# Full matrix products issued as 32- or 64-column tiles when the tensor array already stands in that form

## The chip, the cores and the metric

The kernel runs on one core of a Trainium2 chip. The metric is device time in microseconds for one execution, the median of several runs. A core has a tensor engine (PE; its weight loads are listed as PEld), a vector engine (DVE), a scalar engine (ACT), GpSimd (POOL) and DMA queues, of which SP issues most. PE multiplies a stationary operand (up to 128 rows by 128 columns, loaded first) with a moving operand (up to 512 columns). The array can also be addressed as tiles: a stationary operand of 32 rows by 128 columns uses one of four row tiles, one of 128 rows by 32 columns one of four column tiles, and tiles that lie side by side can work at the same time. In the profile's rows the shape of the stationary operand stands after the names, as in `128*32`. That shape, rounded up to 32, 64 or 128 each way, is called the *form* of the array below.

## The reference

Two layers over 2048 tokens (2 sequences of 1024) of 256 numbers, all float32. Each layer is `x = x + s * g`, where s and g are two branches of the normalized x.

```python
x = L0_attn_x
xn = _layernorm(x, axis=-1)
s = _L0_attn_ref(xn, ...)          # 16 heads of 16, 8 shared keys and values, softmax
g = _silu(_L0_ffn_ref(xn, ...))    # gate and up to 688, weights are picks from a table of 16
x = x + s * g
xn = _layernorm(x, axis=-1)
s = _L1_attn_ref(xn, ...)          # recurrence: state = (1 - w) * state + k v, y = r state
g = _silu(_L1_ffn_ref(xn, ...))    # 8 experts of 176, top 2 per token, and a shared one of 352
x = x + s * g
```

## The kernel before

The whole program is one list of small steps. Each step is a letter, and the string ORDER (lines 78 to 100) says by hand in which order the steps are issued; every engine runs its instructions in that order. So PE's work is one fixed sequence, in which products of different stages stand side by side. There is no loop at run time and no scheduler.

*Layer 0, to about 548 us.* Attention works with keys and queries turned so that a head takes a slot of 32 rows. For each unit of work four heads are handled. `largest` (letter m, L309) multiplies query and key in a 32*128 row tile, and DVE takes the largest (L316). `weigh` (w, L340; L332 for the first eight units) makes the scores in row tiles, and ACT takes their exponentials (L344). `gather` (v, L368; L357 for the first) multiplies the exponentials with the values in four 128*32 column tiles, one for each head, all into one PSUM bank. Around them stand full products and transposes: `turn_x`, `turn_k`, `turn_q`, `divide`, `turn_c` (transposes, L207, L255, L287, L386, L401), `qkv` (L218, 512 columns), `project` (L410, 256 columns). POOL meanwhile decodes the picked weights (L270 and L274). Eight PSUM banks are handed out in turn (`bank`), so that a product waits until DVE or ACT has read the bank that it gets. From about 407 us on the feed-forward branch comes in as well: `gate_up0` (L559, and L541 for the last, shared block; 512 columns) and `down0` (L575; 6 products of 256 columns for a block of 128 tokens).

*Layer 1, from about 575 us.* The recurrence is made in blocks of 128 tokens, four to a step n. `project` and `values` (L1132 with 512, L1159 with 256 columns) make its inputs; `diagonal` (L1186) is in row tiles of 64*128; `level` (L1228) does seven doubling steps, each with 128*64 column tiles of 64 moving columns, and between two levels DVE updates the operands rd and kT (L1235, L1241) and folds the results into w (L1266); `states` and the first half of `reads` (L1298, L1324) are 128*64 tiles too, the second half (L1335) is 64*64. `result` (L1351) is a full product. The router's `logits` (L725) are four 128*32 tiles. `gate_up_s` (L750) is the shared expert's gate and up: three blocks of 128, 128 and 96 channels with 512 columns; `down_s` (L1051) its second product, 256 columns. `route` finds for each expert tile who goes there; its step `ids` (L924) is 32 full products of only 39 moving columns, each behind a comparison `at` on DVE (L913, two buffers). Then come 39 expert tiles: fetch (POOL, L963), a transpose (L975), gate and up (L990), a transpose (L1009), down (L1018), and a scatter to memory (POOL, L1031). At the end `collect`, `combine` and `finish` read the scattered rows, add them up on DVE (L1065) and write out.

A float32 product is two matmul records in the profile. The records of a group of tiles that run together start within some 20 ns of one another.

Of the kernel before, what the change touches and what calls it, by code (L numbers as in the profile page):

```python
# [18 lines left out]
P = 128  # L19
# [5 lines left out]
E = 256  # L25
# [36 lines left out]
NFS = len(FS)  # L62

# [10 lines left out]
C_ALL = C_PRIO + NE  # L74

# [27 lines left out]
def attention(  # L103
    nc, tc, st, b0, small, singles, xs, xnT, s_sb, wlut, ident, epst,
# [24 lines left out]
    for k in range(4):  # L129
        nc.tensor.matmul(bank(f"none_{k}"), xnT[:, 0, 0:P], xnT[:, 0, 0:512], start=True, stop=True)  # L130
# [71 lines left out]
    def turn_x(t):  # L202

        ps = bank(f"xnTp_{t}")
        for kc in range(KC):
            for k in range(2):
                nc.tensor.transpose(  # L207
                    ps[:, (2 * kc + k) * P : (2 * kc + k + 1) * P], xns[t + k][:, ts(kc, P)], ident
                )
        nc.scalar.copy(xnT[:, :, t * P : (t + 2) * P], ps.rearrange("p (k s) -> p k s", k=KC))  # L210
# [3 lines left out]
    def qkv(t):  # L214
        b, c = divmod(t, CPB)
        ps = bank(f"qkv_{t}")
        for kc in range(KC):
            nc.tensor.matmul(  # L218
                ps, xnT[:, kc, ts(t, P)], wqkv[:, kc, :], start=(kc == 0), stop=(kc == KC - 1)
            )  # L220
        qk = ps[:, 0:384].rearrange("p (h d) -> p h d", d=8)
        cs = att2.tile([P, 2, 2, HS, 8], F32, tag="cs", name=f"cs_{t}")
        nc.vector.tensor_tensor(
            cs.rearrange("p w a h d -> p w (a h) d"),
            qk.unsqueeze(1).to_broadcast([P, 2, 2 * HS, 8]),
            rope[:, :, c, :].unsqueeze(2).to_broadcast([P, 2, 2 * HS, 8]),
            ALU.mult,
        )
        nc.scalar.copy(vpads[b][:, c, :, 0:HD], ps[:, 384:512].rearrange("p (k d) -> p k d", d=HD))
        turned[t] = cs[:, 0], cs[:, 1]  # L230
# [17 lines left out]
    def turn_k(t):  # L248

        b, c = divmod(t, CPB)  # L250
        pk = bank(f"kTp_{t}")
        pkv = pk.rearrange("p (j k s) -> p j k s", j=2, k=2)
        for j in range(2):
            for k in range(2):
                nc.tensor.transpose(pkv[:, j, k, :], knat[(c + k) % 4][:, ts(j, 4), :], ident)  # L255
        nc.scalar.copy(kTs[b][:, :, c * P : (c + 2) * P], pk.rearrange("p (j s) -> p j s", j=2))
# [25 lines left out]
    def turn_q(tag, g, h):  # L282

        b, T = divmod(g, NQT)
        ps = bank(f"{tag}p_{g}_{h}")
        for c in range(BC):
            nc.tensor.transpose(ps[:, ts(c, P)], qns[b][:, T, BC * h + c], ident)  # L287
        qT = att2.tile([P, 512], F32, tag=tag, name=f"{tag}_{g}_{h}")
        nc.scalar.copy(qT, ps)
        qTs[tag, g, h] = qT  # L290

    def turn_first(c):

        if c == 0:
            qTs["qTb", 0, 0] = att2.tile([P, 512], F32, tag="qTb", name="qTb_0_0")
        ps = bank(f"qTbp_0_{c}_0")
        nc.tensor.transpose(ps[:, 0:P], qns[0][:, 0, c], ident)
        nc.scalar.copy(qTs["qTb", 0, 0][:, ts(c, P)], ps[:, 0:P])

    def largest(n, i):  # L300

        g, u = divmod(n, 16)
        b, T = divmod(g, NQT)
        c, half = divmod(u, 2)
        if (g, c) not in tops:
            tops[g, c] = att2.tile([P, 2, 4], F32, tag="top", name=f"top_{g}_{c}", bufs=4)
        at = slice(SLOT * i, SLOT * (i + 1))
        ps = bank(f"mx_{n}_{i}")
        nc.tensor.matmul(  # L309
            ps,  # L310
            qTs["qTa", g, c // BC][at, ts(c % BC, P)],
            kTs[b][at, T // 2, ts(half, 512)],
            start=True,
            stop=True,
        )
        nc.vector.tensor_reduce(tops[g, c][:, half, i : i + 1], ps, AX.X, ALU.max)  # L316
        done[g, c] = done.get((g, c), 0) + 1
        if done[g, c] == 8:
            top = tops.pop((g, c))
            nc.vector.tensor_tensor(qns[b][:, T, c, :, HD], top[:, 0, :], top[:, 1, :], ALU.max)  # L320

    def weigh(n, i):

        g, u = divmod(n, 16)
        b, T = divmod(g, NQT)
        h, c = divmod(u, 8)
        at = slice(SLOT * i, SLOT * (i + 1))
        ps = bank(f"sc_{n}_{i}")
        if n < 8:

            for k in range(4):
                nc.tensor.matmul(  # L332
                    ps[:, ts(k, P)],
                    kTs[0][at, 0, ts(c % 2 * 4 + k, P)],
                    qTs["qTb", 0, 0][at, ts(c // 2, P)],
                    start=True,
                    stop=True,
                )
        else:
            nc.tensor.matmul(  # L340
                ps, kTs[b][at, T // 2, ts(c, P)], qTs["qTb", g, h][at, :], start=True, stop=True
            )
        e = att2.tile([P, 512], F32, tag="e", name=f"e_{n}_{i}", bufs=EB)
        nc.scalar.activation(e, ps, AF.Exp, scale=1.0 / math.sqrt(E))  # L344
        es[n, i] = e

    def gather(n):
# [6 lines left out]
        if n < 8:  # L354
            for k in range(4):
                for i in range(4):
                    nc.tensor.matmul(  # L357
                        cxs[0, 0][SLOT * i : SLOT * (i + 1), ts(c // 2, P)],
                        values(0, c % 2 * 4 + k, i),
                        es[n, i][:, ts(k, P)],  # L360
                        start=(c % 2 == 0 and k == 0),
                        stop=(c % 2 == 1 and k == 3),
                    )
        for i in range(4):
            if n < 8:
                es.pop((n, i))
                continue
            nc.tensor.matmul(  # L368
                cxs[g, h][SLOT * i : SLOT * (i + 1), :],
                values(b, c, 4 * (T // 2) + i),  # L370
                es.pop((n, i)),
                start=(c == 0),
# [7 lines left out]
    def divide(g, h):  # L380
# [4 lines left out]
        for c in range(BC):  # L385
            nc.tensor.transpose(ps[:, ts(c, P)], ct[:, ts(c, P)], ident)  # L386
# [11 lines left out]
    def turn_c(t):  # L398
        ps = bank(f"cTp_{t}")
        for kc in range(KC):  # L400
            nc.tensor.transpose(ps[:, ts(kc, P)], s_sb[:, t, ts(kc, P)], ident)  # L401
# [4 lines left out]
    def project(t):  # L406
        cT = cTs.pop(t)
        po = bank(f"so_{t}")
        for kc in range(KC):
            nc.tensor.matmul(  # L410
# [28 lines left out]
def two_layer_kernel(  # L439
# [69 lines left out]
    def transpose_block(srcs, name):  # L509

        ps = bank2(name)
        for kc in range(KC):
            for k, s in enumerate(srcs):
                nc.tensor.transpose(ps[:, kc, ts(k, P)], s[:, ts(kc, P)], ident)
# [3 lines left out]
    singles = []  # L518
    ffw = ctx.enter_context(ExitStack())
# [16 lines left out]
    def gate_up0(n, f, which):  # L536
        if f == FB:

            ps = bank1(f"gt0_{n}")
            for kc in range(KC):  # L540
                nc.tensor.matmul(  # L541
# [16 lines left out]
        for kc in range(KC):  # L558
            nc.tensor.matmul(  # L559
# [11 lines left out]
    def down0(n, k):  # L571
        t = n * BC + k
        po = bank1(f"d0_{t}")
        for f in range(NF0):
            nc.tensor.matmul(  # L575
# [23 lines left out]
    def late_loads(part):  # L599
# [8 lines left out]
        nc, tc, att, b0, small, singles, xs, xnT, s_sb, wlut, ident, epst,  # L608
# [16 lines left out]
    def weights_of_decays():  # L625
        ps = bank1("wxwp")
        psv = ps.rearrange("p (k d) -> p k d", k=KC)
        for kc in range(KC):
            for k in range(KC):
                nc.tensor.matmul(  # L630
# [21 lines left out]
    singles.clear()  # L652
    more_hidden(ffw.enter_context(tc.tile_pool(name="h1", bufs=1, side="right")))
# [19 lines left out]
    wgs = shp.tile([P, KC, 2 * SH_CH], F32, name="wgs")  # L673
# [47 lines left out]
    def logits(n):  # L721
        ps = bank1(f"logits_{n}")
        for kc in range(KC):
            for k in range(BC):
                nc.tensor.matmul(  # L725
                    ps[SLOT * k : SLOT * (k + 1), 0:P],
                    gate[:, kc, :],
                    xnT[:, kc, ts(n * BC + k, P)],
                    start=(kc == 0),
# [15 lines left out]
    def gate_up_s(n, f):  # L745
        lo, sz = FS[f]
        ps = bank2(f"gus_{n}_{f}")
        for which in range(2):
            for kc in range(KC):
                nc.tensor.matmul(  # L750
                    ps[:sz, which, :],
                    wgs[:, kc, which * SH_CH + lo : which * SH_CH + lo + sz],
# [32 lines left out]
    def top_two(n):  # L785
# [3 lines left out]
        def turn_l():  # L789
            ps = bank1(f"lgp_{n}")  # L790
            nc.tensor.transpose(ps[:, 0:P], lgT[n], ident)
# [18 lines left out]
    def route():  # L810
# [29 lines left out]
        def rank():  # L840
            flat = both.rearrange("p c e -> p (c e)")
            ps = bank1("rank")
            nc.tensor.matmul(ps[:, 0:P], before, flat, start=True, stop=True)
            nc.tensor.matmul(ps[:, P : 2 * P], all1, flat, start=True, stop=True)
# [75 lines left out]
        def ids(c):  # L920
            if c == 0:
                whop.append(bank1("who"))
            for k in range(2):
                nc.tensor.matmul(  # L924
# [46 lines left out]
    def turn_x(i):  # L971
        ps = bank1(f"xgTp_{i}")
        xg = tiles.pop(("x", i))
        for kc in range(KC):
            nc.tensor.transpose(ps[:, ts(kc, P)], xg[:, ts(kc, P)], ident)  # L975
# [7 lines left out]
    def gate_up(i):  # L983
# [5 lines left out]
        for kc in range(KC):  # L989
            nc.tensor.matmul(  # L990
                ps[:, 0 : 2 * EI],
                xT[:, kc, :],
                late["gu"][:, kc, bass.ds(e * (2 * EI), 2 * EI)],
                start=(kc == 0),
# [10 lines left out]
    def turn_h(i):  # L1005
        ps = bank1(f"hgTp_{i}")
        h = tiles.pop(("h", i))
        for k in range(2):
            nc.tensor.transpose(ps[:EH, ts(k, P)], h[:, ts(k, EH)], ident)  # L1009
# [4 lines left out]
    def down(i):  # L1014
        ps = bank1(f"dne_{i}")
        e, hT = tiles.pop(("e", i)), tiles.pop(("hT", i))
        for k in range(2):
            nc.tensor.matmul(  # L1018
                ps[:, 0:E],
                hT[:, k, :],  # L1020
                late["d"][:, k, bass.ds(e * E, E)],
                start=(k == 0),
# [20 lines left out]
    def down_s(n, k, m):  # L1043
# [5 lines left out]
        for c in range(m):  # L1049
            for f, (lo, sz) in enumerate(FS):  # L1050
                nc.tensor.matmul(  # L1051
# [75 lines left out]
    def project(n, what_):  # L1127
        wt = {"a": wxw, "r": w1[:, :, 0, :], "k": w1[:, :, 1, :]}[what_]
        pp = bank2(f"{what_}p_{n}")
        for m in range(KC):  # L1130
            for kc in range(KC):
                nc.tensor.matmul(  # L1132
# [19 lines left out]
    def values(n, k):  # L1152
# [4 lines left out]
        for k2 in range(2):  # L1157
            for kc in range(KC):
                nc.tensor.matmul(  # L1159
# [15 lines left out]
    def diagonal(n, m):  # L1175
# [7 lines left out]
        for c in range(BC):  # L1183
            for par in range(2):
                at = half(par)
                nc.tensor.matmul(  # L1186
# [13 lines left out]
    def level(n, lev):  # L1200
# [11 lines left out]
        for c in range(BC):  # L1212
            for pr in range(KC):
                for hf in range(2):
# [10 lines left out]
                    else:  # L1225
                        continue
                    w_ = P if m == HALF else HALF
                    nc.tensor.matmul(  # L1228
                        ps[half(at), w_ * q : w_ * (q + 1)], kd[:, pr, src], to, start=True, stop=True
# [45 lines left out]
    def turn_k(n):  # L1275
        kd = B_[n, "k"]
        pt = bank2(f"kTp_{n}")
        for c in range(BC):
            for m in range(KC):
                nc.tensor.transpose(  # L1280
# [8 lines left out]
    def states(n):  # L1289
# [4 lines left out]
        for c in range(BC):  # L1294
            for m in range(KC):
                for par in range(2):
                    ch = slice(P * m + 64 * par, P * m + 64 * (par + 1))
                    nc.tensor.matmul(  # L1298
                        puv[half(par), c, m, :], ke[:, c, ch], v[:, c, ch], start=True, stop=True
# [16 lines left out]
    def reads(n):  # L1316
# [3 lines left out]
        for c in range(BC):  # L1320
            for m in range(KC):
                for par in range(2):
                    ch = slice(P * m + 64 * par, P * m + 64 * (par + 1))
                    nc.tensor.matmul(  # L1324
                        pyv[half(par), m, c, :],
                        v[:, c, ch],
                        w[:, c, m, par, :],
                        start=(c == 0),
                        stop=False,
                    )  # L1330
        for c in range(BC):
            for m in range(KC):
                for par in range(2):
                    at = half(par)
                    nc.tensor.matmul(  # L1335
# [10 lines left out]
    def result(n, k):  # L1346
        po = bank1(f"s1_{n}_{k}")
        pov = po.rearrange("p (k d) -> p k d", k=2)
        for k2 in range(2):
            for m in range(KC):  # L1350
                nc.tensor.matmul(  # L1351
# [110 lines left out]
def _arrays(i):  # L1462
# [27 lines left out]
    gs = np.concatenate([i["L1_ffn_shared_gate"], i["L1_ffn_shared_up"]], axis=0)  # L1490
# [43 lines left out]
```

## Time and profile before

| what | value |
|---|---|
| time, median of 3 runs | 979.56 us (979.51 to 980.02) |
| the profiled execution | 980.91 us, span 979.0 us |
| matmul records of PE | 6716 |
| granted clock, mean | 0.994 |

The page gives busy time of each engine, a chain of waits followed back from the end, and groups of instructions: line, engine, operation, output and inputs, shapes, count, then busy time, mean length of one in ns, and the idle time of the engine just before them with what ended it. A few groups of PE, told apart by shape, show the products that the change touches and the tiles beside them:

```profile
L368 PE MATMUL cx<-e,vpad 128*32 128x512 f32 x960 | 123.9, 603 | 0.0
L559 PE MATMUL gu<-xnT,wlut 128*128 128x512 f32 x160 | 72.8, 597 | 0.0
L575 PE MATMUL d<-wlut,h 128*128 128x256 f32 x192 | 44.1, 381 | 0.5 <-ACT s_sb L413 0.5
L1228 PE MATMUL lev<-rd,kT 128*64 128x64 f32 x768 | 27.7, 224 | 2.6 <-DVE kT L1241 2.4
L924 PE MATMUL who<-inside,at 128*128 128x39 f32 x64 | 8.4, 279 | 0.1
```

The mean length of a record is not what it costs: records are pipelined and overlap, and their ends are modelled. What a record costs is read from the start of one to the start of the next.

### The profile page before, as it was taken

How to read it: one execution, taken by the hardware profiler on the slowest of the kernel's cores; microseconds unless marked ns; L12 is line 12 of the kernel's file. 1: busy time of each engine (PE TensorE's matmuls, PEld its weight loads, DVE VectorE, ACT ScalarE, POOL GpSimd, SP SyncE). 2: the span in 40 equal slices, each digit the busy share in tenths (PEclk: the TensorE clock that was granted, in tenths of full speed). 3: DMA queues.
4: the chain of work that ended last, by engine and by line, in shares of the span. 5: the costliest groups of instructions: out<-in, count | busy, mean ns of one | idle time of the engine just before them, and what ended most of it. 6: DMA issues, size and time to landing. Idle time of an engine off the chain costs nothing.

```text
span 979.0 us, 17252 instructions
## 1 busy us (share of the span) xinstructions
PE 953.0 (97%) x6716; PEld 522.4 (53%) x6716; DVE 627.9 (64%) x1228; ACT 533.8 (55%) x1009; POOL 586.7 (60%) x485
## 2 busy tenths in 40 slices
PE   8999999999999999999999999999999999999974
PEld 4685433343333443443435475755457677777763
DVE  5898887887767767765760134466877635721993
ACT  4545856566675675766767545527323544464221
POOL 7999999999999999999902020202002355453243
PEclk9999999999999999999999999999999999999998
DMA  5000000000000000000000031003501122221232
GB/s 175 2 2 13 1 12 1 1 12 1 12 2 1 12 1 13 1 1 1 1 1 1 1 122 40 24 1 101 164 1 33 50 66 63 68 76 50 77 119 87
DMA packets 17864, 34.53 MB, mean 35 GB/s; under 512 B 2893, under 2 KB 11231, under 8 KB 17439
## 3 DMA queue, kind: packets, MB, share of 16 engines
q1 hardware_dynamic: 13527, 21.96, 7.1%
q0 software_dynamic: 3968, 10.80, 3.6%
q8 instruction: 54, 0.88, 0.4%
q10 hardware_dynamic: 288, 0.66, 0.2%
q14 instruction: 27, 0.22, 0.1%
HBM read 22.01 MB, written 11.40 MB: 34 GB/s over the span
## 4 chain that ended last, share of the span: by engine, by line
PE 91%; DVE 5%; issue 1%; DMA 1%; POOL 1%; ACT 0%; POOLq 0%; SPq 0%; ACTq 0%; DVEq 0%
PE sc L340 15%; PE mx L309 14%; PE cx L368 12%; PE gu L559 7%; PE gue L990 5%; PE d L575 4%; PE gus L750 4%; PE dne L1018 3%; PE qkv L218 3%; PE lev L1228 3%; PE sc L332 2%; PE rp L1132 1%; PE so L410 1%; PE vp L1159 1%; PE kp L1132 1%; PE ap L1132 1%
## 5 line engine op out<-in xcount | busy, mean ns | idle before, releaser
L316 DVE TENSOR_REDUCE top<-mx 128x1 f32<-128x512 f32 x512 | 324.7, 683 | 92.7 <-PE mx L309 61.7
L344 ACT ACTIVATE e<-sc 128x512 f32<-128x512 f32 x512 | 271.9, 605 | 139.3 <-PE sc L340 65.4
L309 PE MATMUL mx<-kT,qTa 32*128 32x512 f32 x1024 | 287.0, 626 | 0.4 <-DVE top L316 0.4
L270 POOL TENSOR_SCALAR pick<-idx,lut 128x544 f32<-128x544 int32 x120 | 252.3, 2102 | 11.3
L340 PE MATMUL sc<-qTb,kT 32*128 32x512 f32 x960 | 257.5, 625 | 0.5 <-DVE top L316 0.5
L274 POOL TENSOR_TENSOR wlut<-wlut,pick 128x544 f32<-128x544 f32 x120 | 160.4, 1337 | 10.0
L309 PEld LDWEIGHTS mx<-kT,qTa 32*128 32x128 f32 x1024 | 102.5, 183 | 66.1 <-DVE top L316 27.3
L340 PEld LDWEIGHTS sc<-qTb,kT 32*128 32x128 f32 x960 | 93.2, 183 | 79.3 <-DVE top L316 26.4
L368 PE MATMUL cx<-e,vpad 128*32 128x512 f32 x960 | 123.9, 603 | 0.0
L585 POOL TENSOR_TENSOR sgt<-s_sb,g 128x256 f32<-128x256 f32 x16 | 11.6, 728 | 161.1 <-ACT g L583 161.1
L963 POOL DMA_INDIRECT xg<-xn_h,who x39 | 39.4, 1009 | 94.8 <-PE s L1351 70.2
L1031 POOL DMA_INDIRECT y_h<-ye,who x39 | 39.9, 1024 | 69.2 <-ACT ye L1026 25.4
L559 PE MATMUL gu<-xnT,wlut 128*128 128x512 f32 x160 | 72.8, 597 | 0.0
L368 PEld LDWEIGHTS cx<-e,vpad 128*32 128x32 f32 x960 | 20.8, 108 | 84.2 <-issue 73.5
L1002 DVE TENSOR_TENSOR sge<-sge,gue 128x176 f32<-128x176 f32 x39 | 13.1, 338 | 73.4 <-ACT sge L1001 73.1
L569 DVE TENSOR_TENSOR h<-sg,gu 128x512 f32<-128x512 f32 x20 | 13.8, 688 | 65.4 <-ACT sg L568 50.3
L990 PE MATMUL gue<-wgu,xT 128*128 x156 | 53.0, 462 | 1.6 <-issue 1.0
L559 PEld LDWEIGHTS gu<-xnT,wlut 128*128 128x128 f32 x160 | 29.1, 190 | 34.0 <-issue 29.9
L575 PE MATMUL d<-wlut,h 128*128 128x256 f32 x192 | 44.1, 381 | 0.5 <-ACT s_sb L413 0.5
L750 PE MATMUL gus<-xnT,wgs 128*128 128x512 f32 (+1 forms) x96 | 43.1, 597 | 0.0
L1018 PE MATMUL dne<-wd,hTe 88*128 x156 | 40.0, 380 | 0.5 <-ACT hTe L1011 0.5
L575 PEld LDWEIGHTS d<-wlut,h 128*128 128x128 f32 x192 | 35.7, 190 | 8.1 <-issue 1.8
(235 smaller groups left out, 1346.6 us busy)
## 6 DMA issues: line engine op xcount, KB each, us to landing
xn_h<-xn SPq DMA_DIRECT2D x16, 256.0 KB, 3.4
yk<-y_h SPq DMA_DIRECT2D x16, 256.0 KB, 3.0
wgu<-in_wgu SPq DMA_DIRECT2D x1, 2816.0 KB, 10.9
idx<-in_idx SPq DMA_DIRECT2D x8, 272.0 KB, 2.7
out_x<-g SPq DMA_DIRECT2D x16, 128.0 KB, 1.7
wd<-in_wd SPq DMA_DIRECT2D x1, 1408.0 KB
xs<-in_x SPq DMA_DIRECT2D x2, 512.0 KB, 4.6
w<-in_w SPq DMA_DIRECT2D x1, 1024.0 KB
```

The source lines that it names most:

```text
L270: nc.gpsimd.tensor_scalar(dst, codes[piece], float(j), lut[:, j : j + 1], ALU.is_equal, ALU.mult)
L274: nc.gpsimd.tensor_tensor(wlut[:, at], wlut[:, at], dst, ALU.add)
L309: nc.tensor.matmul(ps, qTs["qTa", g, c // BC][at, ts(c % BC, P)], kTs[b][at, T // 2, ts(half, 512)], start=True, stop=True,)
L316: nc.vector.tensor_reduce(tops[g, c][:, half, i : i + 1], ps, AX.X, ALU.max)
L340: nc.tensor.matmul(ps, kTs[b][at, T // 2, ts(c, P)], qTs["qTb", g, h][at, :], start=True, stop=True)
L344: nc.scalar.activation(e, ps, AF.Exp, scale=1.0 / math.sqrt(E))
L368: nc.tensor.matmul(cxs[g, h][SLOT * i : SLOT * (i + 1), :], values(b, c, 4 * (T // 2) + i), es.pop((n, i)), start=(c == 0), stop=(c == CPB ...
L559: nc.tensor.matmul(hT0[which], wlut[:, lo + kc * P :][:, 0:P], xnT[:, kc, ts(n, 512)], start=(kc == 0), stop=(kc == KC - 1),)
L575: nc.tensor.matmul(po[:, 0:E], hidden(n)[:, f, ts(k, P)], wd0[:, f, :], start=(f == 0), stop=(f == NF0 - 1),)
L750: nc.tensor.matmul(ps[:sz, which, :], wgs[:, kc, which * SH_CH + lo : which * SH_CH + lo + sz], xnT[:, kc, ts(n, 512)], start=(kc == 0), s ...
L990: nc.tensor.matmul(ps[:, 0 : 2 * EI], xT[:, kc, :], late["gu"][:, kc, bass.ds(e * (2 * EI), 2 * EI)], start=(kc == 0), stop=(kc == KC - 1),)
L1018: nc.tensor.matmul(ps[:, 0:E], hT[:, k, :], late["d"][:, k, bass.ds(e * E, E)], start=(k == 0), stop=(k == 1),)
```

## The change

A small class, Array, now issues nearly all products, and remembers the form in which the last one left the array. A product with no width of its own takes the width of the last column tiles (`form`); behind a row tile, where nothing is remembered, it takes `narrow`, 32 in layer 0 and 64 in layer 1. If the width is less than 128, the product is issued as four or two column tiles side by side, with the same moving operand, into the same bank. Row tiles (`rows`) forget the form, transposes set it to 128. The experts' products (L990, L1018) and the four products ahead of everything (L130) have the width 128 written out; cx, logits, lev, add and y (from w) keep their widths of 32 or 64. A full product behind full products or a transpose stays as it was.

The third block of `gate_up_s` becomes 128 channels wide instead of 96; the weights get 32 columns of zeros at their end, and the extra rows of the result are not read. ORDER, the other engines' work and all buffers but wgs are the same.

```diff
+SH_PAD = NFS * P - SH_CH
...
+class Array:
+    def __init__(self, nc, narrow):
+        self.nc, self.narrow, self.form = nc, narrow, None
+
+    def rows(self, out, lhsT, rhs, start=True, stop=True):
+        self.form = None
+        self.nc.tensor.matmul(out, lhsT, rhs, start=start, stop=stop)
+
+    def matmul(self, out, lhsT, rhs, start, stop, width=None):
+        if len(lhsT.shape) > 2:
+            lhsT = lhsT.rearrange("p a b -> p (a b)")
+        w = self.form = width or self.form or self.narrow
+        for i in range(0, out.shape[0], w):
+            self.nc.tensor.matmul(out[i : i + w], lhsT[:, i : i + w], rhs, start=start, stop=stop)
+
+    def transpose(self, out, in_, ident):
+        self.form = P
+        self.nc.tensor.transpose(out, in_, ident)
...
-        nc.tensor.matmul(bank(f"none_{k}"), xnT[:, 0, 0:P], xnT[:, 0, 0:512], start=True, stop=True)
+        te.matmul(bank(f"none_{k}"), xnT[:, 0, 0:P], xnT[:, 0, 0:512], start=True, stop=True, width=P)
...
-            nc.tensor.matmul(
+            te.matmul(
                 ps, xnT[:, kc, ts(t, P)], wqkv[:, kc, :], start=(kc == 0), stop=(kc == KC - 1)
             )
...
-        nc.tensor.matmul(
+        te.rows(
             ps,
             qTs["qTa", g, c // BC][at, ts(c % BC, P)],
             kTs[b][at, T // 2, ts(half, 512)],
...
-            nc.tensor.matmul(
+            te.matmul(
                 cxs[g, h][SLOT * i : SLOT * (i + 1), :],
                 values(b, c, 4 * (T // 2) + i),
                 es.pop((n, i)),
+                width=SLOT,
...
+    te = Array(nc, SLOT)
...
     att.close()
     singles.clear()
+    te.narrow, te.form = HALF, None
...
-    wgs = shp.tile([P, KC, 2 * SH_CH], F32, name="wgs")
+    wgs = shp.tile([P, KC, 2 * SH_CH + SH_PAD], F32, name="wgs")
...
-                nc.tensor.matmul(
-                    ps[:sz, which, :],
-                    wgs[:, kc, which * SH_CH + lo : which * SH_CH + lo + sz],
+                te.matmul(
+                    ps[:, which, :],
+                    wgs[:, kc, which * SH_CH + lo : which * SH_CH + lo + P],
                     xnT[:, kc, ts(n, 512)],
...
-                nc.tensor.matmul(
+                te.matmul(
                     whop[0][:, 0:NTILE],
                     at[c][:, k, :],
                     inside[:, 2 * c + k, :],
...
-            nc.tensor.matmul(
+            te.matmul(
                 ps[:, 0 : 2 * EI],
                 xT[:, kc, :],
                 late["gu"][:, kc, bass.ds(e * (2 * EI), 2 * EI)],
+                width=P,
...
-                    nc.tensor.matmul(
-                        ps[half(at), w_ * q : w_ * (q + 1)], kd[:, pr, src], to, start=True, stop=True
+                    te.matmul(
+                        ps[half(at), w_ * q : w_ * (q + 1)], kd[:, pr, src], to, start=True, stop=True, width=HALF
                     )
...
-    gs = np.concatenate([i["L1_ffn_shared_gate"], i["L1_ffn_shared_up"]], axis=0)
+    gs = [i["L1_ffn_shared_gate"], i["L1_ffn_shared_up"], np.zeros((SH_PAD, E), np.float32)]
+    gs = np.concatenate(gs, axis=0)
```

The other products change in the same way: transposes call `te.transpose`; L332, L340, L1186 and L1335 call `te.rows`; L410, L541, L559, L575, L630, L843, L844, L1051, L1132, L1159 and L1351 call `te.matmul` without a width; L357 and L725 with 32; L1018 with 128; L1298 and L1324 with 64.

## The prediction

> **What bounds the kernel now.** First the page: busy time, and the chain of work that ended last.
>
> ```profile
> PE 953.0 (97%) x6716; PEld 522.4 (53%) x6716; DVE 627.9 (64%) x1228; ACT 533.8 (55%) x1009; POOL 586.7 (60%) x485
> ...
> PE 91%; DVE 5%; issue 1%; DMA 1%; POOL 1%; ACT 0%; POOLq 0%; SPq 0%; ACTq 0%; DVEq 0%
> ```
>
> TensorE is 91% of the chain. A "busy" PE is not yet a PE at its peak, so next the windows by stage (columns: busy us of PE, weight load, DVE, ACT, POOL, then granted clock and DMA), cut where the work changes:
>
> ```profile
> 0.00:548.00 548.00, 543.87 (x3932) 242.38 (x3932) 390.01 (x684) 352.80 (x661) 466.78 (x352) 1.00 0.04 12
> ...
> 600.00:722.00 122.00, 122.00 (x624) 71.07 (x623) 79.13 (x224) 57.64 (x78) 12.35 (x21) 1.00 0.20 62
> 722.00:753.00 31.00, 29.90 (x293) 23.48 (x292) 21.06 (x50) 9.01 (x14) 3.95 (x4) 1.00 0.05 15
> 753.00:915.00 162.00, 161.40 (x1262) 118.36 (x1263) 76.30 (x147) 78.63 (x189) 73.41 (x72) 1.00 0.20 60
> 915.00:947.00 32.00, 25.17 (x244) 20.60 (x242) 30.57 (x47) 5.31 (x13) 10.88 (x12) 1.00 0.39 124
> 947.00:979.00 32.00, 19.14 (x168) 16.03 (x168) 15.81 (x35) 8.15 (x16) 11.35 (x14) 0.83 0.25 83
> ```
>
> From 600 to 915 us PE is full and nothing else is. From 915 to 947 DVE is full (30.57 of 32). Before 548 PE is full by this count, but its passes, drains and entries as worked out below add up to 482 us only: it shares the pace with DVE and ACT.
>
> Then the timeline of PE, for what a change of form costs (start, us, what, count of records). A float32 product is two records, "passes" here; four 32-wide or two 64-wide tiles that start together are one pass.
>
> ```profile
> 417.33 1.07 PE L368 MATMUL cx<-e,vpad 128*32 128x512 f32 x8
> 418.33 1.98 PE L559 MATMUL gu<-xnT,wlut 128*128 128x512 f32 x4
> 420.24 0.69 PE L309 MATMUL mx<-kT,qTa 32*128 32x512 f32 x1
> ```
>
> ```profile
> 709.04 1.89 PE L1159 MATMUL vp<-w,x2T 128*128 128x256 f32 x8
> 710.77 3.60 PE L750 MATMUL gus<-xnT,wgs 128*128 128x512 f32 x8
> 714.29 1.15 PE L1228 MATMUL lev<-rd,kT 128*64 128x64 f32 x32
> 715.38 7.11 PE L750 MATMUL gus<-xnT,wgs 128*96 128x512 f32 x16
> 722.32 0.98 PE L924 MATMUL who<-inside,at 128*128 128x39 f32 x8
> ...
> 724.25 1.08 PE L924 MATMUL who<-inside,at 128*128 128x39 f32 x8
> 725.17 1.10 PE L750 MATMUL gus<-xnT,wgs 128*128 128x512 f32 x2
> ```
>
> Take differences of starts, not the modelled lengths. vp (same form before and after): 1.73 us for 8, 0.216 a pass of 256 columns. gus x16: 6.94 us, of which 16 x 0.427; the rest, 0.10, is its first weight load, which nothing covers just after a change of form. gus x8, entered from its own form and left for another: 3.52 = 8 x 0.428 + 0.095. So a change costs a **drain of 0.095 us** and an **entry**: 0.104 for a 128-wide product. Check on gu: 1.91 = 4 x 0.428 + 0.095 + 0.104. The entry shrinks with the width: cx x8 is two passes, 1.00 = 2 x 0.429 + 0.02 (stagger of four starts) + 0.095 + 0.024, so **0.024** for 32 columns; lev and y (739.21 to 741.10: 1.89 = 16 x 0.109 + 0.095 + 0.051) give **0.051** for 64; transposes have **0.057** (406.81 to 407.30: 0.49 for four at 0.109).
>
> **The change part by part.**
>
> *1. Streaming in tiles: zero.* By walking the 6716 records in order with the new rule for the form, 116 passes become 32-wide (72 of 512 columns, 44 of 256: 72 x 0.429 + 44 x 0.216 = 40.4 us) and 292 become 64-wide (116 and 176: 87.8 us), besides 48 of who. The cx rows stream 512 columns in four 32-wide tiles at 0.429, as the full array does; the y rows stream 128 columns in 64-wide pairs at 0.109, as a full transpose. No row shows a 64-wide pair at 256 or 512 columns, or tiles that share one moving operand. Bounds: 0, and rival B's price; I take 0, by cx and y. Nothing is gained below 0, since the moving columns are the same.
>
> **A rule against this.** The Trainium skill, "TensorE: Matmul & The Clock Gate", Part 3 on packing small matmuls, says that a weight load overlaps running matmuls only where its row group differs. All column tiles here have the same rows, so by the rule every tiled pass would show its load: 116 x 0.024 + 292 x 0.051 = +17.7 us, and the kernel would be slower. The cx rows say otherwise: if each pass of cx showed its load, the 1.00 above would be 1.02, and cx x16 (403.88 to 405.74, 1.86) would be 1.93; four passes at 0.429 + 0.02 + 0.024 + 0.095 is 1.855. The trace decides for 32 columns; for 64 the y and lev rows do, at few columns.
>
> *2. Changes of form: 390 now, 360 after.* 38 go (full product beside a tile: 0.199 where the full product came second, 0.146 or 0.119 where a 64- or 32-wide tile did), 8 come (a transpose behind a product that is now tiled, +0.152), 9 only get narrower (a full product between row tiles: 0.104 to 0.024, so 0.080). The expert products and all transposes stay full, and the row tiles of mx and sc stay: most changes stay with them.
>
> *3. who, 39 columns.* A full pass takes 0.112 ((725.17 - 724.25 - 0.024)/8), bound by its 128-column load. A 64-wide pair should take lev's step, 0.058 ((1.09 - 0.095 - 0.051)/16). 48 of the 64 passes fall behind lev, y or add and become pairs: 48 x 0.054 = 2.6 us. Bounds: 0 and 2.6; I take 2.6, lev being the same width and nearly as short.
>
> *4. Padding.* The third block of gus goes from 96 to 128 columns: no change of pass (0.427 before too). wgs grows by 32 columns of 704, in a load behind others at 578 us, used at 684: hidden. Some 700 more PE records dispatch 7 ns apart within a group: hidden behind passes of 0.2 us and more.
>
> **By stage**, with what hides it:
>
> - 0 to 548: 11 gone, 1 come, 7 narrower: 9 x 0.199 + 2 x 0.119 + 7 x 0.080 - 0.152 = 2.44. Does it pass? mx and sc restart after each block and wait for DVE and ACT to free banks:
>
> ```profile
> L316 DVE TENSOR_REDUCE top<-mx 128x1 f32<-128x512 f32 x512 | 324.7, 683 | 92.7 <-PE mx L309 61.7
> L344 ACT ACTIVATE e<-sc 128x512 f32<-128x512 f32 x512 | 271.9, 605 | 139.3 <-PE sc L340 65.4
> ```
>
>   Both sit idle for PE (the two rows' last columns), and at the end of nearly all changed blocks they are idle or in their last instruction; but four blocks end with 0.3 to 0.6 us of backlog. I take 80%: -1.95 (ends 0 and -2.44). POOL's decoding (to 488.7) is used much later.
> - 548 to 600: 2 gone, 2 come, one of these behind a wait for ACT at 575.5: -0.1.
> - 600 to 722: 10 gone, 2 come: 7 x 0.199 + 3 x 0.146 - 2 x 0.152 = 1.53. PE is full: -1.53 passes.
> - 722 to 753: who 2.59, 4 gone (2 x 0.146 + 2 x 0.119), 2 come (0.304): -2.82. The who at 732.99 is followed by transposes and then waits at 734.94 for DVE's at, whose start hangs on the end of gus, not of who; that block's 0.28 is lost: -2.54.
> - 753 to 915: mostly forced full; 2 gone, 0.199 + 0.146: -0.35. PE is full.
> - 915 to 947: 8 gone, 4 x 0.199 + 4 x 0.146 = 1.38 on PE, but each lev here waits for DVE (kT L1241), which is full. I count 0.
> - 947 to the end: one gone, one come, one narrower (0.104 to 0.051): -0.10.
>
> Sum: -6.57. On the profiled execution's 980.91 (span 979.0) that is 974.3 (972.4); on the median shown, 979.56, **973.0 us**. The profile is 1.35 above the median, and I apply the difference to both.
>
> **One thing that the sum leaves out: the clock.** The vp at 948.13 takes 3.42 us against 1.89 at 709.04; the granted clock fell to half at 947.6 after 3.1 us without PE work. With faster ds the gap grows by up to 0.2 us and the phase shifts: another such spell costs, or saves, about 1.6.
>
> **Rivals.**
>
> A. *The attention stage absorbs its part* (banks late from DVE 683 ns and ACT 605 ns each), and half of who waits for DVE's at: -6.57 + 1.95 + 1.2 = -3.4, **976.1**. For it: DVE and ACT are busy 390 and 353 of 548. Against: their idle time is on PE. 20%.
>
> B. *Slower: tiled passes show their weight load*, most of all the 64-wide ones, which no row shows at these lengths. Place: all 292 passes at 0.051, +14.9: **987.9**; with the 32-wide also, +17.7: 990.7. It decides from 6.57/292 = 22 ns a pass (about 7% of 87.8 us). Slower reading of a shared moving operand would look the same. Against: cx, y, lev. 11%.
>
> C. *It doesn't do what it says*: savings and added switches cancel, or the tiles are taken one after another at the edges: **979**, 5%.
>
> **Chances.** Forecast 61%, A 20%, B 11%, C 5%; 3% for still faster. The range: everything passes (-8.6: 970.9), with some clock luck 970.5; A with a lost clock spell, 977.0. What a measurement here can tell from no change is 0.2%, 2.0 us: faster (under 977.6) 0.83, within 0.06, slower 0.11.
>
> **What would show it.** 418.33: gu in 128*32, x16, with cx + gu in 2.71 instead of 2.91. gus in 128*64 at 0.43 a pair: right; at 0.48: B. who as pairs, eight passes in about 0.6 instead of 0.91. 30 fewer changes of form. PE weight-load count up by some 700. The lev at 946.90 about 6.5 earlier and still waiting for DVE. If the stretch up to 548 shortens by less than 0.5 us, A is right. The forecast is wrong if 64-wide pairs don't start within 10 ns of each other.

## The result, and the profile after

| | before | after |
|---|---|---|
| median, us | 979.88 (979.51 to 982.18, 6 runs) | 976.82 (976.26 to 977.28, 6 runs) |
| profiled execution; span | 980.91; 979.0 | 977.04; 975.3 |
| matmul records; changes of form | 6716; 390 | 7404; 360 |

The ratio is 0.996, 95% interval 0.9947 to 0.9972: faster by 3.1 us. The forecast was 973.0, so the direction and the range held (976.8 lies at its slow end, 977.0), and the gain was half of the 6.57 that the sum gave. Executions of before range from 979.3 to 982.3 us, beside the first experiments in two groups around 979.7 and 982.1, so that a median can lie in either, and gains are read below from the traces of one profiled execution each. The page after, the same two lines as before:

```profile
PE 947.2 (97%) x7404; PEld 502.6 (52%) x7404; DVE 628.8 (64%) x1228; ACT 534.0 (55%) x1009; POOL 587.5 (60%) x485
...
PE 91%; DVE 6%; issue 1%; POOL 1%; ACT 0%; POOLq 0%; ACTq 0%; DVEq 0%
```

In the code after, all products are issued by lines 88, 95 and 99 of the class, so rows are told apart by their names. The timeline of PE after, around the block that stood at 417.33 to 420.24:

```profile
417.29 1.07 PE L95 MATMUL cx<-e,vpad 128*32 128x512 f32 x8
418.17 1.90 PE L95 MATMUL gu<-xnT,wlut 128*32 128x512 f32 x16
420.00 0.69 PE L88 MATMUL mx<-kT,qTa 32*128 32x512 f32 x1
```

cx and gu take 2.71 us from start to start, where they took 2.91: the drain of 0.095 and the entry of 0.104 are gone, and gu's four passes in tiles take 0.429 each as before. In layer 1, 64-wide:

```profile
706.71 1.90 PE L95 MATMUL vp<-w,x2T 128*64 128x256 f32 x16
708.44 3.60 PE L95 MATMUL gus<-xnT,wgs 128*64 128x512 f32 x16
711.87 1.10 PE L95 MATMUL lev<-rd,kT 128*64 128x64 f32 x32
712.80 0.60 PE L95 MATMUL gus<-xnT,wgs 128*64 128x512 f32 x2
```

vp: 1.73 for 8 passes of 256 columns (0.216); gus: 3.43 for 8 of 512 (0.429), with no drain of 0.095 at its end; lev: 0.93 instead of 1.09. So what no row of before showed, 64-wide pairs at these lengths with one moving operand, streams at full rate. The local costs are right; the question is what became of them. The two programs issue the same blocks in the same order, so each block's start after can be set against its start before. This is the lead so found (negative is earlier):

| block, us before | lead, us | part of the sum up to there |
|---|---|---|
| xnTp, 12 | -0.06 | 0 |
| rows at 298.2 | -0.79 | |
| rows at 393.2 | -0.07 | |
| rows at 518.0 | -0.04 | -1.52 on PE, 80% counted |
| rows at 547.5 | -0.97 | -1.95 |
| gu at 599.6 | -1.20 | -2.05 |
| first who, 722.3 | -2.65 | -3.58 |
| who at 734.9 | -3.41 | |
| s at 744.8 | -2.81 | -6.12 |
| dne at 916.7 | -3.00 | -6.47 |
| lev at 946.9 | -2.90 | -6.47 |
| end | -3.8 | -6.57 |

Three places differ: the lead won before 490 us comes and goes and is nothing at 518; who's gain is won and then lost between 735 and 745; and the end gains 0.9 where 0.1 was counted.

### The profile page after: what moved, and what is told of

Read it like the earlier page. It is cut to its first block, busy times and chain, and to the rows that moved or that the text cites. A ratio compares the mean times of both kernels' runs of the same rounds, so it can differ in the third digit from the quotient of the medians.

```text
span 975.3 us, 18628 instructions
## 1 busy us (share of the span) xinstructions
PE 947.2 (97%) x7404; PEld 502.6 (52%) x7404; DVE 628.8 (64%) x1228; ACT 534.0 (55%) x1009; POOL 587.5 (60%) x485
## 4 chain that ended last, share of the span: by engine, by line
PE 91%; DVE 6%; issue 1%; POOL 1%; ACT 0%; POOLq 0%; ACTq 0%; DVEq 0%
PE sc L88 16%; PE mx L88 14%; PE cx L95 13%; PE gu L95 7%; PE gue L95 5%; PE d L95 4%; PE gus L95 4%; PE dne L95 3%; PE qkv L95 3%; PE lev L95 2%; PE kp L95 1%; PE rp L95 1%; PE ap L95 1%; PE so L95 1%; DVE top L341 1%; DVE w L1298 1%
## 5 line engine op out<-in xcount | busy, mean ns | idle before, releaser
L88 PE MATMUL sc<-qTb,kT 32*128 32x512 f32 (+1 forms) x1216 | 286.1, 552 | 0.8 <-DVE top L341 0.8
L88 PEld LDWEIGHTS sc<-qTb,kT 32*128 32x128 f32 x1216 | 118.9, 184 | 81.9 <-DVE top L341 28.6
L95 PE MATMUL cx<-e,vpad 128*32 128x512 f32 (+1 forms) x1216 | 132.1, 533 | 0.0
L95 PEld LDWEIGHTS cx<-e,vpad 128*32 128x32 f32 x1216 | 27.8, 108 | 86.3 <-issue 74.6
L95 PE MATMUL gu<-xnT,wlut 128*32 128x512 f32 (+2 forms) x320 | 72.2, 592 | 0.0
L95 PE MATMUL d<-wlut,h 128*128 128x256 f32 (+2 forms) x300 | 43.8, 379 | 0.5 <-ACT s_sb L440 0.5
L95 PEld LDWEIGHTS gu<-xnT,wlut 128*32 128x32 f32 (+2 forms) x320 | 25.3, 137 | 36.1 <-issue 35.0
L95 PE MATMUL gus<-xnT,wgs 128*64 128x512 f32 (+2 forms) x184 | 42.8, 593 | 0.0
L1298 DVE COPY_PREDICATED w<-msk,lev 64x512 f32<-64x512 int32 x40 | 37.9, 948 | 0.7
```

The costliest lines, as they stand in the source:

```text
L88: self.nc.tensor.matmul(out, lhsT, rhs, start=start, stop=stop)
L95: self.nc.tensor.matmul(out[i : i + w], lhsT[:, i : i + w], rhs, start=start, stop=stop)
L1298: nc.vector.copy_predicated(wv[at, :, hf], msk[at, lev, ts(hf, HALF // 2)] .rearrange("p (n s) -> p n s", s=m) .unsqueeze(1) .to_broadcast ...
```

## Experiments

### What takes the lead in attention

The lead of -0.43 that PE has at 430.6 is still there on DVE and ACT at 437.0, and 0.05 a moment later. Timelines of before and of after at that place (start, us, engine, what; the rows of DVE and POOL):

```profile
436.60 1.34 POOL L274 TENSOR_TENSOR wlut<-wlut,pick 128x544 f32<-128x544 f32 x1
437.03 0.93 DVE L320 TENSOR_TENSOR qn<-top 128x4 f32<-128x4 f32 x1
437.88 1.28 DVE L316 TENSOR_REDUCE top<-mx 128x1 f32<-128x512 f32 x2
```

```profile
436.55 1.34 POOL L299 TENSOR_TENSOR wlut<-wlut,pick 128x544 f32<-128x544 f32 x1
436.60 1.31 DVE L345 TENSOR_TENSOR qn<-top 128x4 f32<-128x4 f32 x1
437.83 1.28 DVE L341 TENSOR_REDUCE top<-mx 128x1 f32<-128x512 f32 x2
```

DVE comes to its maximum of 4 numbers a row at 437.03 before and 0.43 earlier after, and both times it is over just as POOL's addition ends (437.94 and 437.89). It takes as long as POOL does, 0.93 and 1.31 us. POOL decodes at its own beat and has no lead. The nine losses of 0.19 us and more that the lead takes between 100 and 490 us all follow within 6 us of a maximum that took over 0.3 us; 28 of the 64 maxima of after did, and 21 of these ended within 25 ns of the end of a POOL addition. Theory 1: this sets DVE, and through the banks PE, back to POOL's beat. Theory 2, the prediction's rival A: the banks come free late because DVE and ACT have a backlog, and POOL has no part.

**The maximum with one operand in SBUF**, in both kernels:

```diff
-            nc.vector.tensor_tensor(qns[b][:, T, c, :, HD], top[:, 0, :], top[:, 1, :], ALU.max)
+            nc.vector.tensor_reduce(qns[b][:, T, c, :, HD], top.rearrange("p h i -> p i h"), AX.X, ALU.max)
```

> The kernel before, with DVE's maximum into qn (L320, two SBUF operands) made by a reduction of one SBUF operand. Theory 1 (in attention DVE is set to POOL's beat: the two-operand maximum waits for the POOL decoding instruction under way, and so gives back any lead of PE): qn takes about 0.2 us every time instead of 0.17 to 1.35, DVE loses some 14 us of stalls in attention, and the kernel gets 2 to 10 us faster. Theory 2 (PE's lead is lost to DVE and ACT freeing the banks late, POOL has no part): the stalls are not on the path, and the time stays within 1 us of before.

> The changed kernel with the same reduction in place of the maximum. Theory 1: against before_reduce the last block of row tiles ahead of 519 us starts 1.2 to 1.8 us earlier (0.04 in after against before), and the whole is 4.2 to 5.2 us faster than before_reduce. Theory 2: the lead there is again under 0.3 us, and the whole is about 3.1 us faster than before_reduce.

before_reduce took 973.10 us, 0.9921 of before (0.9907 to 0.9935), whose median beside it was 981.79; after_reduce 967.83, 0.9864 (0.9847 to 0.988). The difference of the two is 5.3 us (4.2 to 5.2 expected) where it was 3.1. The 8.7 us of the medians are too much for what the line gave, since this median of before lies in the upper of its two groups and that of before_reduce in the lower of its own (973.0 and 975.1): group against group it is 6.7 and 7.0. Groups of DVE by shape (busy us, mean ns), before and with the reduction:

```profile
L320 DVE TENSOR_TENSOR qn<-top 128x4 f32<-128x4 f32 x64 | 26.0, 407 | 2.2
```

```profile
L320 DVE TENSOR_REDUCE qn<-top 128x4 f32<-128x8 f32 x64 | 10.5, 164 | 2.2
```

64 calls lose 15.5 us, and before_reduce leads before by 7.0 at 518 us. Its lead comes only up to 490, as long as POOL decodes. after_reduce leads before_reduce by 0.98 at the block that stood at 518.0 (the last row tiles ahead of 519), less than the 1.2 expected, and by 1.91 at the one at 547.5, against 0.04 and 0.97. The prediction's PE sums were 1.52 and 2.44.

Of the 0.54 that is missing up to 518, 0.40 was lost at one place, at 152 us. There the lead of 0.38 fell to nothing behind another DVE instruction, the one into xn. Before_reduce and after_reduce:

```profile
149.20 1.35 POOL L274 TENSOR_TENSOR wlut<-wlut,pick 128x544 f32<-128x544 f32 x1
150.27 0.43 DVE L199 TENSOR_SCALAR xn<-xs,mv_a,rstd_a 128x256 f32<-128x256 f32 x1
```

```profile
149.21 1.35 POOL L299 TENSOR_TENSOR wlut<-wlut,pick 128x544 f32<-128x544 f32 x1
149.88 0.83 DVE L224 TENSOR_SCALAR xn<-xs,mv_a,rstd_a 128x256 f32<-128x256 f32 x1
```

It came 0.39 earlier, while POOL's addition still ran, took 0.83 instead of 0.43, and was over at the same time.

A caution for reading such leads: the first 12 us, in which the loads arrive, differ from run to run by up to 1.2 us, and most of that shift stays (in after_l1 below, 0.83 of 1.13 at 60 us). So a lead is read against the one at 12 us (0.01 in this pair) or at 60, which leaves some tenths in doubt where the shift is large.

**POOL idle instead**, with the maximum as it was:

```diff
     def decode(piece, j):
+        if j:
+            return
```

> The kernel before, with 15 of the 16 picks of each piece of decoded weights left out (so POOL is idle for most of attention; layer 0's feed-forward weights are not the reference's). Theory 1 (the stalls of the maximum into qn are POOL's): with POOL idle the maximum takes 0.17 us every time, although it still has two SBUF operands, and attention is about 7 us shorter than before, as in before_reduce. Theory 2 (before_reduce is faster since the reduction is in itself a better instruction): qn still has calls of over 0.3 us.

> The changed kernel with the same picks left out. Theory 1: at 548 us of before's clock it leads before_nodec by 1.8 to 2.5 us (the prediction's sum for this stage was 2.44, after_reduce had 2.2); Theory 2: by about 1.0, as after has against before.

One execution each: 972.58 and 967.13 us. In before_nodec the maximum, with its two operands, is short again:

```profile
L322 DVE TENSOR_TENSOR qn<-top 128x4 f32<-128x4 f32 x64 | 10.7, 167 | 2.2
```

So the operand form alone costs nothing; POOL beside it does. The xn of 150 us takes 0.40 in both runs. before_nodec leads before by 8.26 us at 547, of which 1.17 was there at 12 us: 7.1, the same as with the reduction. after_nodec leads before_nodec by 0.77 and 1.70 at the two blocks; 1.70 is just short of the 1.8 expected. Without the difference at the start (it was 0.59 behind at 60 us) that is 1.36 and 2.29, where after has 0 and 0.9. Theory 1 holds in both pairs. For theory 2 little is left: with POOL idle 1.36 of the counted 1.52 came through before 518, and most of what the reduction's pair lacks was lost at xn, to POOL as well.

The Trainium skill says this outright: "SBUF — State Buffer", section "Who interferes with whom", has a DVE instruction with two SBUF inputs contend with a GpSimd instruction that reads SBUF, one blocking the other for a whole instruction, and one with a single SBUF input, outside the modes that use two ports, not. The runs agree for the maximum (0.93 and 1.31 us held, 0.164 not). The prediction should have read it: it called POOL's decoding "used much later" and stopped there.

### What takes who's gain

A first part is lost at the second block, 724.25 in before, in all three pairs: the block ahead of it gives 0.47, and PE then waits as long for the comparison `at`. In after:

```profile
721.60 0.77 PE L95 MATMUL who<-inside,at 128*64 128x39 f32 x16 [0.42 <-DVE at L943]
```

The larger part is lost from 735 on. Timelines of PE before and after:

```profile
737.11 1.15 PE L1298 MATMUL add<-v,ke 128*64 128x64 f32 x32
738.19 1.08 PE L924 MATMUL who<-inside,at 128*128 128x39 f32 x8
739.21 1.97 PE L1324 MATMUL y<-w,v 128*64 128x128 f32 x32
```

```profile
730.10 1.09 PE L99 MATMUL kTp<-cst,kT 128*128 128x128 f32 x8
731.53 2.24 PE L95 MATMUL who<-inside,at 128*128 128x39 f32 x16 [0.34 <-DVE at L943]
733.70 1.78 PE L95 MATMUL add<-v,ke 128*64 128x64 f32 x32
735.27 1.03 PE L95 MATMUL who<-inside,at 128*64 128x39 f32 x16
736.09 2.57 PE L95 MATMUL y<-w,v 128*64 128x128 f32 x32
```

add takes 1.78 instead of 1.15, y 2.57 instead of 1.97. A window over just that time (PE, weight load, DVE, ACT, POOL, then the granted clock) says why:

```profile
733.97:737.39 3.42, 3.42 (x60) 3.42 (x56) 2.12 (x10) 0.00 (x0) 0.00 (x0) 0.50 0.02 5
```

PE's clock was halved for 3.41 us, and this cost 1.6. Two ways to test it: a third buffer for the comparisons that who waits for, and who kept full.

```diff
-            at[c] = rt_two.tile([P, 2, P], F32, tag="at", name=f"at_{c}")
+            at[c] = rt_two.tile([P, 2, P], F32, tag="at", name=f"at_{c}", bufs=3)
```

> The changed kernel with three buffers instead of two for the comparisons (at) ahead of who. Theory A (the gain of who's tiles is lost because PE then waits for at, which waits for a free buffer, and this idling brings on the half-clock spell of 3.4 us at 734 us): the waits ahead of who shrink, no half-clock spell between 715 and 750, and the kernel is 0.8 to 2 us faster than after. Theory B (DVE's own order of work, not the buffers, makes at late): within 0.4 us of after, and the spell stays.

```diff
                 te.matmul(
                     whop[0][:, 0:NTILE],
                     at[c][:, k, :],
                     inside[:, 2 * c + k, :],
+                    width=P,
```

> The changed kernel with the 39-column products (who) kept full, which also leaves the form at 128 behind them. By the prediction's sum it should lose 2.6 us of who and about 0.3 of changes of form: 979.5. If that gain is lost anyway to waits and to the clock spell: within 0.6 us of after, and no half-clock spell near 734 us.

after_at3: 975.72 us, 0.9944 (0.993 to 0.9957), 1.1 below after. Its timeline at the same place:

```profile
731.50 1.98 PE L95 MATMUL who<-inside,at 128*128 128x39 f32 x16 [0.34 <-DVE at L943]
733.40 1.15 PE L95 MATMUL add<-v,ke 128*64 128x64 f32 x32
734.39 0.62 PE L95 MATMUL who<-inside,at 128*64 128x39 f32 x16
734.83 1.95 PE L95 MATMUL y<-w,v 128*64 128x128 f32 x32
```

The spell is gone: add, who and y together take 3.30 instead of 4.89 (from add's start to the end of y's passes at 738.59 and 736.70), 1.6 us. But the wait for `at` was hardly less: the lead at add is 0.30. So the expectation's effect came, and only a part of its reason: the buffers saved 0.3, and the rest is that the spell fell away. Why such a small step took it away is not shown. In both runs these are the 3.41 us ahead of 733.97, after and then after_at3 (columns as above):

```profile
730.56:733.97 3.41, 3.00 (x30) 2.60 (x30) 2.69 (x7) 2.07 (x3) 0.00 (x0) 1.00 0.00 0
```

```profile
730.56:733.97 3.41, 3.07 (x40) 2.79 (x40) 2.83 (x7) 2.07 (x3) 0.00 (x0) 1.00 0.00 0
```

Of the 1.9 us that after_at3 is ahead of after by the block s, and 2.0 by 916, the end keeps 0.9: its profile has spells at 928.5 and 942.2 instead, and the second lies on the last block's lev and vp, where the lead falls. after_reduce bears out that the spell, not the buffers, is what counts: with two buffers as in after, but 8 us earlier, it has a granted clock of 1.00 from 715 to 745, and adding the third buffer to it (after_reduce_at3, below) moved this stage by 0.26.

after_whofull: 977.66, 0.9964 (0.9951 to 0.9977), 0.8 above after, a little over the 0.6 expected and far from the 2.6. It has no spell at 734. Against after it falls back by 0.90 from the first who to the one at 734.9, and then regains 0.59 up to s, where after has its spell. So who's tiles do save time, and in after one spell took nearly all of it: from the first who to s, who and changes of form together, after_reduce gains 1.77 on before_reduce and after_nodec 1.77 on before_nodec, neither with a spell there, where 2.54 was counted; after gains 0.16, and the difference is the 1.6 of the spell. after_l1, below, has a spell at the same place, so it is more than an accident of one execution.

### The parts alone

```diff
-        w = self.form = width or self.form or self.narrow
+        w = self.form = width or (P if self.narrow == HALF else self.form or self.narrow)
```

That keeps the change to layer 0 (after_l0); with SLOT for HALF it is kept to layer 1 (after_l1).

> The change in layer 0 alone; in layer 1 every product without a width is full. Theory 1 (POOL's beat takes every lead before 490 us, what comes after passes): the lead on before is under 0.1 us at 515 us, 0.9 to 1.1 at 548 and 1.2 to 1.4 at 575, and stays so to 900. The time is 0.8 to 1.8 us below before. By the prediction's sum it would be 2.0.

> The change in layer 1 alone; in layer 0 every product without a width is full. No lead up to 575 us, -1.4 to -1.6 at 722. Then who: with no half-clock spell between 715 and 750, -3.0 to -3.4 at 745; with one, -1.3 to -1.9. The time is 1.5 to 4 us below before, and the two parts' leads at 722 add up to after's 2.65 to within 0.2.

after_l0: 979.88 us, ratio 0.9988 (0.9982 to 0.9995). Its lead is 0.20 at 12 us, 0.16 at 518, 1.08 at 547, 1.42 at 574 and 1.28 at 900. Less the 0.20, that is nothing, 0.9, 1.2 and 1.1, within 0.1 of the expected; the time, 0.5 below before, is less than the 0.8 to 1.8. after_l1: 977.43, 0.9962 (0.9948 to 0.9976), 3.0 below. It has a lead of 0.84 at 60 us and 0.86 at 574, which is the start's and not the change's; the expectation of none did not think of that. Less this it has 1.27 at the gus at 715, 1.34 at the first who (1.4 to 1.6 expected) and 1.49 at s, with a spell at 734.8 as in after. With after_l0's 1.16 at 715 the parts give 2.43, and after had 2.51.

### The two remedies together, and the end

> The changed kernel with both the reduction and the third buffer. The two act at different places (before 490 us, and 715 to 750 us), but after_reduce had no half-clock spell near who, which was most of what the third buffer took away. So not the sum of 9.0 and 1.1: 966.5 to 967.6, 0.2 to 1.3 us faster than after_reduce.

967.44 us, 0.9864 (0.9848 to 0.9881): within the expectation, and not told apart from after_reduce's 967.83. Both beat before and after clearly.

At the end PE waits for DVE ahead of the last doubling step, and the clock falls. Timelines of before and of after:

```profile
946.90 1.30 PE L1228 MATMUL lev<-rd,kT 128*64 128x128 f32 x16 [3.13 <-DVE kT L1241]
948.13 3.42 PE L1159 MATMUL vp<-w,x2T 128*128 128x256 f32 x8
```

```profile
944.00 1.09 PE L95 MATMUL lev<-rd,kT 128*64 128x128 f32 x16 [3.21 <-DVE kT L1273]
944.93 1.90 PE L95 MATMUL vp<-w,x2T 128*64 128x256 f32 x16
947.66 1.10 PE L99 MATMUL kTp<-cst,kT 128*128 128x128 f32 x8 [0.84 <-DVE kT L1273]
```

In before the half-clock spell (from 947.65) lay on vp, 3.26 us to the next block; in after there was none here, vp took 1.9, and then kTp waited for DVE: 2.73 in all. lev to vp is 0.3 shorter, of which 0.2 is the change of form. That is 0.8 of the 0.9 that the end gained. To take the spell away on purpose, six products whose result is not read were put into the gap, on after_reduce_at3:

```diff
+        if n == NBLK - 1 and lev == NLEV - 1:
+            keep_on = bank1("keep_on")
+            for k in range(6):
+                te.matmul(keep_on[:, 0:E], ident, w1[:, 0, 0, :], start=True, stop=True)
         ps = bank1(f"lev_{n}_{lev}")
```

> after_reduce_at3 with six products of 256 columns, whose result is not read, ahead of the last doubling step of the last block, where PE waits 3 us for DVE (2.6 us of work in that gap). If the half-clock spell at the end comes from that idling and costs about 1.6 us: no spell there, and 0.8 to 1.6 us faster than after_reduce_at3. If the spell is off the path or comes from another gap: within 0.3 us, or slower by what the products delay.

967.29 us against 967.44: the medians show no difference. The spell after the gap did go, but vp, now 1.93, was followed by a wait:

```profile
929.83 2.76 PE L95 MATMUL keep_on<-w,cst 128*64 128x256 f32 x24
933.01 1.09 PE L95 MATMUL lev<-rd,kT 128*64 128x128 f32 x16 [0.42 <-DVE kT L1277]
933.91 1.93 PE L95 MATMUL vp<-w,x2T 128*64 128x256 f32 x16
937.16 1.09 PE L99 MATMUL kTp<-cst,kT 128*128 128x128 f32 x8 [1.33 <-DVE kT L1277]
```

From lev to kTp it is 4.15 us here and 4.62 in after_reduce_at3, where the spell lay on lev and vp: DVE's kT is next on the path, at nearly the time at which a half-clock vp ends. This profile also had another spell, at 919.6. What a spell at this place costs is therefore nearer to 0.5 than to the 1.6 of the prediction.

## Why the prediction was half right

- **Prices and count.** 390 to 360 changes, 7404 records, drain 0.095, entries 0.024 and 0.051, passes in tiles at full rate, padding and dispatch at nothing: each as predicted. Rival B (tiled passes show their weight load) is out: a 64-wide pass of 512 columns takes 0.429. The trace decides against the skill's rule as the prediction read it, for 64 columns too.
- **0 to 548 us, -1.95.** Measured -0.97, all of it after 515. The failed step is "POOL's decoding (to 488.7) is used much later", with the 80% that rests on it: it looked at POOL's results and not at POOL running beside DVE. Before 490 POOL's decoding sets the beat, and a lead on PE lasts until one of DVE's maxima meets a POOL addition. Rival A named the right place and the wrong engine. With POOL out of the way the stage gives 1.9 and 2.3 of the 2.44 on PE, about what the step counted.
- **548 to 722, -1.63.** Measured -1.68 by the table.
- **722 to 753, -2.54.** Measured -0.2. The step failed in three places. A wait for `at` at 724.25 takes 0.47, where only the one at 734.94 was counted. The saving of a pass was put at 54 ns throughout: a pair takes 55 ns and a full pass 115 in the blocks behind a tile, but 100 in the three blocks behind a full product (0.699 us from the first to the last of eight), which makes up about 0.3. Together these turn 2.54 into the 1.77 measured where no spell fell. In after a half-clock spell takes the other 1.6. The prediction named such a spell as a risk, but only at the end.
- **753 to 947, -0.35.** Measured -0.1 (-0.2 up to 916, where the pairs with the reduction and without POOL have -0.36 and -0.35), and the tail's 1.38 on PE was rightly put at 0: lev waits for DVE.
- **The end, -0.10.** Measured -0.9: the spell that before has on vp is not there in after. This is luck.
- **Rival A's time**, 976.1, is the nearest to the measured one, by luck: its banks play no part that the runs show, its waits for `at` are 0.47 of the 1.2 that it put on them, and the spell at 734 and the gain at the end are not in it.

## What to carry to other kernels

Summing local prices is sound where one engine is full; where engines share the pace, ask which one has a beat of its own, and which instruction of the others must wait for it. A small DVE instruction with two SBUF operands beside a busy POOL is worth rewriting to one operand: here one line gave 7.0 us, over twice what the change itself gave. Check a gain against where the clock spells fell in both profiles before believing its last microsecond.

## What was not expected of the hardware

- A 4-element DVE maximum took up to 1.345 us beside POOL, and 0.17 without it. The scaling into xn, with one tensor and two columns of scalars, was held too: up to 1.41 us, where with POOL idle most calls take 0.40 and none over 0.71.
- The half-clock spell at 734 us in after followed a stretch in which PE was idle for 0.41 us of 3.41 only, and otherwise had transposes and 39-column full products in flight. In after_at3 PE was idle for 0.34 of it, with 40 records instead of 30, and no spell followed. The two runs are within 0.03 us of each other up to this place, and their clocks change in step: all spells that end before the last one, and all stretches between two spells, last a multiple of 3.413 us, and after_at3's at 928.51 comes 57 times that after 733.97. So the moment does not explain the difference between the two; what in the stretch brought the spell on stays open.
- A pair of 64-wide tiles with 39 columns takes 55 ns where a full pass takes 100 to 115. A full pass is about as long as the entry of 0.104 us, the first weight load laid open, so narrow tiles also shorten products whose weight load is longer than their columns.
